# Two attention and feed-forward layers: tokens in tiles of 128 between the first attention and the experts

## The chip, the cores and the metric

The kernel runs on one core of a Trainium2 chip. Time is device time in microseconds (us). The core has a matrix engine (PE, with its weight loads shown as PEld), a vector engine (DVE), a scalar engine (ACT), a general engine (POOL), and SP, which does no arithmetic and issues transfers. ACT and POOL issue transfers too. Each engine works through its own instructions in the order in which the program emits them, and waits on semaphores for the others.

## The reference, cut to what matters

There are 16 batches of 112 tokens with 256 values, and a context of 375 rows per batch. Four stages are added to `x` in turn, each on a layernorm of it:

```python
x = x + xattn0(_layernorm(x), ctx)          # 16 heads of 64, softmax, then @ Wo + bo
x = x + ffn0(_layernorm(x))
x = x + xattn1(_layernorm(x), ctx, ctx, mask)   # one head of 256, softmax over 375
x = x + ffn1(_layernorm(x))                 # int8 product, one scale for all tokens

# ffn0
top1 = argmax(softmax(xf @ gate_w.T))       # 2 experts
masked = xf[None] * one_hot(top1).T[:, :, None]
h = relu(einsum('end,edh->enh', masked, w1) + b1[:, None, :])
routing = (einsum('enh,ehd->end', h, w2) + b2[:, None, :]).sum(0)
shared = relu(xf @ sw1 + sb1) @ sw2 + sb2   # hidden width 1024
return routing + shared
```

The expert that a token doesn't take sees zeros, so it adds a constant row, `relu(b1) @ w2 + b2`. The kernel makes those rows once (`crow`). Everything is in float32 but the last product. The scale of that product needs the maximum over all tokens, so nothing of it can begin before the last token's layernorm.

## The kernel before

**Units.** The first attention is cut into 64 units, `u = 4 * batch + k`, of four heads each (`unit`, L1007). A unit makes scores for itself (`scores`, L374), subtracts the maximum and exponentiates on ACT (`exps`, L394), divides on POOL (`divide`, L405), and in the next unit transposes the probabilities in 32x32 blocks on DVE (`unit_T`, L428) and moves the blocks between partitions by twelve transfers, on SP in most units (`unit_move`, L437). Three units later PE multiplies them with `v` (`weighted`, L462) and DVE copies the result into `oT`. Keys of the next unit and values of the unit two back are made in between (`make_kT`, `make_v`). `ctxT`, the transposed context of a batch, has three buffers.

**Work between units.** Lists `extra` and `middle` are filled by `at(u, ...)` and `mid(u, ...)` (L911 to L998) and are emitted at the end and in the middle of unit u. That written schedule sets the order on every engine. Small chains of vector work, such as a layernorm (`norm`, L241), are handed out one step at a time by `pump` while other work is emitted, and `finish` emits what is left of one.

**From attention to experts.** All activations lie in `xall`, 112 tokens of a batch on the partitions and one column block per batch. When a batch's heads are done, `attention_out` (L489) multiplies by Wo (`po`), adds to x and starts the layernorm `l1`; `ffn_turn` transposes it. `shared` (L702) runs the shared feed-forward for two batches at a time, 224 columns, eight groups in all. It runs eight hidden blocks f, each with two `ph` products and, two blocks behind, `acc` products (`Rows`, L655).

For the routed part, tokens are sorted by expert through DRAM. `sort_gate` finds the expert, `sort_place` works out the row by counting (a matmul with a triangle of ones), and `sort_put` scatters the rows with an indirect transfer. Tokens of expert 0 fill a set from the front and those of expert 1 from the back, leaving one spare slot between them, so that each slot of rows has one expert. There are three sets (`SORTED`, L48): batches 0 to 7 in 8 slots of 128 rows, 8 to 13 in 7 slots of 112, and 14 and 15 in 3 slots of 112. `sort_counts` gives each slot's expert, `slot_weights` reads it on SP (`value_load`) and loads that expert's two weight matrices of 1 MB each, double buffered; `slot_rows`, `slot_turn`, `slot_run` and `slot_store` take a slot through the expert. `sort_get` gathers a batch's rows back on POOL with the same places and `sort_add` adds them to x.

**Where the stages lie.** Slots of the first set run in units 39 to 46, with shared groups 0 to 5 in units 12 to 52, and the second attention of batches 0 to 7 is spread over units 49 to 59 (`second_1` to `second_4`, then `third`). The second set runs from step 64 to 70, the third from 71 to 73, with shared group 6 at 67 and 70. From step 75 the second attention of batches 8 to 15 is pipelined over steps (`stages`, L1084), with a quarter of shared group 7 in each of the first four; each batch is gathered four steps ahead. `keep_warm` puts idle matmuls into the last steps. Then the scale is formed and the int8 product and the output follow (L1132 on).

Of the kernel before, what the change touches and what calls it, by code (L numbers as in the profile page):

```python
# [19 lines left out]
P = 128  # L20
B, S, D = 16, 112, 256
SK = 375
# [23 lines left out]
POOL_PLACES = 7  # L46

SORTED = ((0, 8, 128), (8, 14, 112), (14, 16, 112))  # L48
# [5 lines left out]
def tile_kernel(  # L54
    ctx: ExitStack,
    tc: tile.TileContext,
    x,
    ctx_in,
# [26 lines left out]
    ctxp = ctx.enter_context(tc.tile_pool(name="ctx", bufs=3))  # L85
# [14 lines left out]
    xall = const.tile([S, B, D], F32, tag="x", name="x")  # L100
    xs = [xall[:, b, :] for b in range(B)]
# [3 lines left out]
    def load_ctx(b):  # L105
        t = late(ctxp, 3, 4, [KC, NKC, D], "ctx_nat", f"ctx{b}")
        nc.sync.dma_start(out=t, in_=ctx_in[b].rearrange("(c p) d -> p c d", p=KC))
        ctx_nat[b] = t
# [5 lines left out]
    def load_ctxT2(b):  # L114
        ctxT2[b] = ctxp.tile([P, DC, SK], F32, tag="ctxT_2", name=f"ctxT2_{b}")
        nc.sync.dma_start(out=ctxT2[b], in_=ctx_t[b])
# [6 lines left out]
    nc.sync.dma_start(out=xall[:, 0:2, :], in_=x[:, 0:2, :])  # L123
# [15 lines left out]
    def more_loads():  # L139
        load_ctxT(1)  # L140
        nc.sync.dma_start(out=xall[:, 2:4, :], in_=x[:, 2:4, :])

    def rest_of_x():
        nc.scalar.dma_start(out=xall[:, 4:, :], in_=x[:, 4:, :])
# [26 lines left out]
    half = const.tile([S, GB], F32, tag="half", name="half")  # L171
# [9 lines left out]
    def row_to_all(src, name):  # L181
        t = const.tile([S, D], F32, tag=name, name=name)
        late_loads[name] = lambda: nc.gpsimd.dma_start(out=t, in_=src.partition_broadcast(S))
        return t
# [56 lines left out]
    def norm(bs, name, on_act=False):  # L241

        n = len(bs)
        mv = small.tile([S, n, 2], F32, tag=f"mv{n}", name=f"mv_{name}_{bs[0]}")
        v = small.tile([S, n], F32, tag=f"var{n}", name=f"var_{name}_{bs[0]}")
        y = small.tile([S, n], F32, tag=f"rs_y{n}", name=f"y_{name}_{bs[0]}")
        steps = []
        for i, b in enumerate(bs):
            st = small.tile([S, 6], F32, tag="bn", name=f"bn_{name}_{b}")
            steps.append(lambda st=st, b=b: nc.vector.bn_stats(st, xs[b]))  # L250
            steps.append(lambda st=st, i=i: nc.vector.bn_aggr(mv[:, i, :], st))  # L251

        def root():
            nc.gpsimd.tensor_scalar(v, mv[:, :, 1], EPS_LN, None, ALU.add)  # L254
            nc.gpsimd.tensor_tensor(y, v, half[:, :n], ALU.pow)
# [4 lines left out]
        def rows(b, i):  # L260
            if name == "l1":
                xn = tmp.tile([S, D], F32, tag="xn1", name=f"xn_{name}_{b}")
# [7 lines left out]
            else:  # L270
                nc.vector.tensor_scalar(
                    xn, xs[b], mv[:, i, 0:1], y[:, i : i + 1], ALU.subtract, ALU.mult
# [5 lines left out]
    def transposed(dst, src, name):  # L278

        pt = gen(f"pt_{name}")  # L280
        for c in range(DC):
            nc.tensor.transpose(
                pt[:, c * S : (c + 1) * S], src[:, c * P : (c + 1) * P], ident[:S, :S]
            )
        nc.scalar.copy(dst, pt[:, : DC * S].rearrange("p (c s) -> p c s", c=DC))
# [43 lines left out]
    def q_norm(g, at_once=False):  # L329
        bs = list(range(g * GB, (g + 1) * GB))  # L330
        steps = norm(bs, "l0")
        if not at_once:
            steps.append(lambda: add_bo(bs))
        chain(("l0", g), steps)
# [3 lines left out]
    def add_bo(bs):  # L338
        for b in bs:
            nc.gpsimd.tensor_tensor(xs[b], xs[b], bo_bc, ALU.add)  # L340
# [29 lines left out]
    probs, pTs, oT = {}, {}, {}  # L370
# [91 lines left out]
    def weighted(u):  # L462
        b, k = divmod(u, UN)
        if k == 0:
            oT[b] = act.tile([P, MC, S], F32, tag="oT", name=f"oT_{b}", bufs=1)
        pa = gen(f"pa_{b}_{k}")
        pT = pTs.pop(u)
        for j2 in range(2):
# [12 lines left out]
        nc.vector.tensor_copy(  # L481
            oT[b][:, 2 * k : 2 * k + 2, :],
            pa[:, : 2 * S].rearrange("p (c s) -> p c s", c=2),
        )


    ffn_in = {}

    def attention_out(b):  # L489
        po = gen(f"po_{b}")  # L490
        for m in range(MC):
            nc.tensor.matmul(  # L492
                po[:S, :D], oT[b][:, m, :], big["wo"][:, m, :], start=(m == 0), stop=(m == MC - 1)
            )
        nc.vector.tensor_tensor(xs[b], po[:S, :D], xs[b], ALU.add)
        chain(("l1", b), norm([b], "l1"))

    def ffn_turn(b):
        g, i = divmod(b, GB)
        if i == 0:  # L500
            ffn_in[g] = tmp.tile([P, DC, GT], F32, tag="ffn_x", name=f"ffn_x_{g}")
        finish(("l1", b))
        transposed(ffn_in[g][:, :, i * S : (i + 1) * S], normed["l1", b], f"x1_{b}")

    def gate_scores(b):
        g, i = divmod(b, GB)
        sl = slice(i * S, (i + 1) * S)
        pg = gen(f"pg_{b}")
        for dc in range(DC):
            nc.tensor.matmul(  # L510
                pg[:S, :2],
                ffn_in[g][:, dc, sl],
                gw_sb[:, dc, :],
                start=(dc == 0),
                stop=(dc == DC - 1),
            )
        gs = small.tile([S, 2], F32, tag="gs", name=f"gs_{b}")
        nc.vector.tensor_copy(gs, pg[:S, :2])
# [3 lines left out]
    def sort_gate(b):  # L522
        s = sort_of[b]
        gs = gate_scores(b)
        nc.vector.tensor_tensor(second[:, b : b + 1], gs[:, 1:2], gs[:, 0:1], ALU.is_gt)

        if b == s.first:
            nc.vector.tensor_copy(seconds[:, b : b + 1], second[:, b : b + 1])
        else:
            nc.vector.tensor_tensor(  # L530
                seconds[:, b : b + 1], seconds[:, b - 1 : b], second[:, b : b + 1], ALU.add
            )

    def sort_place(b):
        s = sort_of[b]
        i = b - s.first
        pr = gen(f"pr_{b}")
        nc.tensor.matmul(
# [716 lines left out]
```

## Time and profile before

| what | us |
|---|---|
| median of 3 runs (1007.63 to 1008.91) | 1008.49 |
| the profiled execution's own time | 1008.94 |
| its span, first to last instruction | 1007.2 |
| PE, PEld busy | 960.2, 737.5 |
| DVE, ACT, POOL busy | 498.8, 470.4, 451.4 |
| start of the last unit's scores | 809.3 |
| end of the last expert slot | 927.1 |
| start of the last stage's wait for all tokens | 978.1 |

The page's time rows of 40 slices show granted PE clock 9 (0.9 or more) in all but one slice, and from 28 to 231 GB/s moved in a slice. Busy times of different engines overlap, so they don't add up to the span. A row of the stage view gives a stretch of the span and how long each engine worked in it. A row of a timeline gives start, length, engine, line, operation and tile; a bracket behind it is the idle time just before and what ended it.

### The profile page before, as it was taken

To read this page: it belongs to the slowest core of one execution; us is meant where nothing else is said; L and a number is where in the kernel's file an instruction comes from. 1 tells how busy PE (TensorE), PEld (TensorE's weight loads), DVE (VectorE), ACT (ScalarE), POOL (GpSimd) and SP (SyncE) were. 2 spreads that over 40 slices of the span, in tenths; PEclk is the share of its full clock that TensorE was granted. 3 is DMA by queue.
4 is the path that set the end of the run, shared out by engine and by line. 5 is a ranking of instruction groups with operands and counts; after the bars stand their busy time and mean duration, and the time that the engine had idled before them with its cause. 6 is when DMAs were issued, how large, how long until landed. Compare 5 with 4: busy or idle time off the path is not lost. (4 is left out here: it accounts for less than half of the span.)

```text
span 1007.2 us, 17359 instructions
## 1 busy us (share of the span) xinstructions
PE 960.2 (95%) x5829; PEld 737.5 (73%) x5829; DVE 498.8 (50%) x1263; ACT 470.4 (47%) x1257; POOL 451.4 (45%) x492
## 2 busy tenths in 40 slices
PE   8999999999999999999999999899999989998874
PEld 5777687778777777877778886667777768887653
DVE  5556735553545455454353335674765632222355
ACT  4756435653565456445344334463455641222353
POOL 4764634662465445453242224663556631013434
PEclk9999999999999999999999999999999989999998
DMA  6657312431333133244554252442433375556622
GB/s 185 165 154 201 86 39 68 99 79 28 77 86 71 39 70 79 45 129 149 163 207 149 93 156 73 125 130 59 130 73 72 77 229 205 187 205 231 199 68 74
DMA packets 117832, 119.68 MB, mean 119 GB/s; under 512 B 15422, under 2 KB 106400, under 8 KB 112384
## 3 DMA queue, kind: packets, MB, share of 16 engines
q1 hardware_dynamic: 107968, 101.53, 35.6%
q10 hardware_dynamic: 7264, 10.74, 3.6%
q0 software_dynamic: 2512, 6.30, 2.1%
q8 instruction: 47, 0.77, 0.3%
q14 instruction: 41, 0.34, 0.1%
HBM read 71.78 MB, written 8.98 MB: 80 GB/s over the span
## 5 line engine op out<-in xcount | busy, mean ns | idle before, releaser
L411 POOL TENSOR_SCALAR p<-p,rden 128x375 f32<-128x375 f32 x256 | 314.4, 1241 | 235.8 <-DVE rden L408 232.4
L399 ACT ACTIVATE p<-sc,nmax 128x375 f32<-128x375 f32 x256 | 143.1, 570 | 183.8 <-DVE nmax L390 179.9
L293 PE MATMUL pk<-ctxT,wk 128*128 128x375 f32 x512 | 191.9, 497 | 5.5 <-ACT kT L302 2.4
L314 PE MATMUL pv<-wv,ctxT 128*128 128x256 f32 (+1 forms) x768 | 186.8, 379 | 0.1
L314 PEld LDWEIGHTS pv<-wv,ctxT 128*128 128x128 f32 (+1 forms) x768 | 142.8, 187 | 47.0 <-ACT kT L302 1.2
L460 ACT COPY pT<-blk 32x384 f32<-32x384 f32 x256 | 130.0, 508 | 25.2 <-DMA pT<-blk 16.8
L432 DVE STREAM_TRANSPOSE blk<-p 128x384 f32<-128x384 f32 x256 | 132.5, 553 | 8.9 <-POOL p L411 4.9
L293 PEld LDWEIGHTS pk<-ctxT,wk 128*128 128x128 f32 x512 | 90.1, 191 | 57.4 <-issue 10.5
L390 DVE TENSOR_REDUCE nmax<-sc 128x2 f32<-128x750 f32 x128 | 111.9, 912 | 0.6 <-PE sc L382 0.4
L472 PEld LDWEIGHTS pa<-pT,v 128*64 128x64 f32 (+1 forms) x1536 | 75.0, 137 | 34.2 <-issue 14.2
L382 PE MATMUL sc<-kT,qT 64*128 64x375 f32 x512 | 98.1, 501 | 0.0
L472 PE MATMUL pa<-pT,v 128*64 128x112 f32 (+1 forms) x1536 | 89.3, 265 | 3.1 <-DVE v L327 2.5
L327 DVE COPY v<-pv 119x256 f32<-119x256 f32 x64 | 27.0, 421 | 116.3 <-PE pv L314 116.3
L302 ACT COPY kT<-pk 128x375 f32<-128x375 f32 x128 | 61.0, 477 | 46.9 <-PE pk L293 46.9
L254 POOL TENSOR_SCALAR var_l<-mv_l 112x1 f32<-112x1 f32 (+1 forms) x56 | 13.5, 240 | 125.2 <-DVE mv_l L251 97.4
L689 DVE TENSOR_SCALAR hT_sl<-ph_sl,slot_b 128x112 f32<-128x112 f32 (+1 forms) x72 | 24.6, 341 | 89.5 <-PE ph_sl L679 87.5
L382 PEld LDWEIGHTS sc<-kT,qT 64*128 64x128 f32 x512 | 43.9, 186 | 32.9 <-issue 11.7
L691 ACT ACTIVATE hT_sl<-ph_sl,slot_b 128x112 f32<-128x112 f32 (+1 forms) x72 | 25.5, 359 | 87.7 <-PE ph_sl L679 74.8
L666 PE MATMUL acc_sh<-sw,hT_sh 128*112 128x256 f32 x256 | 62.8, 380 | 3.5 <-ACT hT_sh L691 3.5
L492 PE MATMUL po<-wo,oT 128*112 128x256 f32 x256 | 57.9, 379 | 0.0
L713 POOL TENSOR_TENSOR x<-x,crow 112x256 f32<-112x256 f32 x16 | 11.3, 725 | 99.4 <-DVE x L710 72.1
L679 PE MATMUL ph_sh<-ffn_x,sw 128*128 128x224 f32 x256 | 55.7, 353 | 0.0
(204 smaller groups left out, 1279.4 us busy)
## 6 DMA issues: line engine op xcount, KB each, us to landing
pT<-blk SPq DMA_DIRECT2D x732, 48.0 KB
ctxT<-in_ctx_t SPq DMA_DIRECT2D x31, 375.0 KB
ctx<-in_ctx SPq DMA_DIRECT2D x16, 375.0 KB
ew<-in_w ACTq DMA_DIRECT2D x2, 1024.0 KB
sw<-in_sw ACTq DMA_DIRECT2D x2, 1024.0 KB
out<-y SPq DMA_DIRECT2D x8, 224.0 KB
pT<-blk ACTq DMA_DIRECT2D x36, 48.0 KB
x<-in_x ACTq DMA_DIRECT2D x1, 1344.0 KB
```

Source lines behind the costliest of these rows:

```text
L293: nc.tensor.matmul(pk[:, :SK], wk_sb[:, dc, m * P : (m + 1) * P], ctxT[b][:, dc, :], start=(dc == 0), stop=(dc == DC - 1),)
L302: nc.scalar.copy(t, pk[:, :SK])
L314: nc.tensor.matmul(pv[: KP[c], n * UD : (n + 1) * UD], ctxT[b][:, dc, c * P : c * P + KP[c]], wv_sb[:, dc, k * UD : (k + 1) * UD], start=( ...
L382: nc.tensor.matmul(sc[:, j, :SK], qT[g, m][r, i * P : (i + 1) * P], kT[b, m][r, :], start=True, stop=True,)
L390: nc.vector.tensor_reduce(nmax, sc[:, :, :SK], AX.X, ALU.max, negate=True)
L399: nc.scalar.activation(p[:, :SK], sc[:, j, :SK], AF.Exp, bias=nmax[:, j : j + 1], accum_out=den[:, j : j + 1])
L411: nc.gpsimd.tensor_scalar(p, p, rden[:, j : j + 1], None, ALU.mult)
L432: nc.vector.transpose(blocked[u][:, :, h * 32 : (h + 1) * 32], probs[u][h].rearrange("p (n k) -> p n k", k=32),)
L460: nc.scalar.copy(pT[r, :, i, :], of[r, :, i, :])
L472: nc.tensor.matmul(pa[j * DH : (j + 1) * DH, j2 * S : (j2 + 1) * S].rearrange("p (i q) -> p i q", q=QB), vv[b, k][: KP[c], c, h * DH : (h ...
L492: nc.tensor.matmul(po[:S, :D], oT[b][:, m, :], big["wo"][:, m, :], start=(m == 0), stop=(m == MC - 1))
L666: nc.tensor.matmul(self.acc[:n, i, :D], hT[:, i * n : (i + 1) * n], self.wb[:, f, :], start=(f == 0), stop=(f == FC - 1),)
```

## The change

Between the first attention's output and the experts, tokens go in 14 tiles of 128 that ignore batch borders. `xall` holds tiles in that part, and batches from the gather on.

- `oT` is a ring of 256 columns. A batch that runs over its end is copied in two pieces. `attention_out`, `ffn_turn`, `sort_gate`, `sort_place` and `sort_put` work on tiles, 14 of each, as soon as the batch that ends a tile is done.
- x is loaded twice: by pairs of batches for the first layernorm (`load_xb`, one buffer, POOL after the first) and by tiles for the residual (`load_xt`, ACT).
- The shared feed-forward runs in seven chunks of 256 columns, taken from a ring of three chunks. Chunks 0 to 3 stand in units 16, 24, 32 and 47, chunks 4 and 5 in quarters in steps 64 to 69, chunk 6 in quarters in the four steps before the second attention. `Rows` carries its two blocks behind from one quarter to the next.
- There are two sets of seven tiles, each with eight slots of 128. First and last slot of a set have a fixed expert. The second set runs in steps 70 to 77 in the order 0, 7, 1, 6, 2, 5, 3, 4; weights of slots 0 and 7 are loaded from unit 58 on, those of the others behind the run two before, and the transpose of a slot is emitted ahead of the run before it.
- Residuals return to batches through DRAM: `shared_store` writes a chunk to `x2_d` (POOL), `load_xs` reads a batch of it (POOL). `places_by_batch` writes the places of a set to DRAM by tile and reads them back by batch, both on SP. `sort_get` uses those.
- `ctxT`, and before the tail `ctxT_2` and `ctx_nat`, have two buffers instead of three; `ctxT` of batch b+2 is loaded at the end of unit 4b+5, not 4b+2.
- The second attention's pipeline begins at step 82 instead of 75.

```diff
-SORTED = ((0, 8, 128), (8, 14, 112), (14, 16, 112))
+NT = B * S // P
+SORTED = ((0, NT // 2), (NT // 2, NT))
+RING = 2 * P
+CHUNK = 2 * P
+KEPT = 3
...
-    ctxp = ctx.enter_context(tc.tile_pool(name="ctx", bufs=3))
+    ctxp = ctx.enter_context(tc.tile_pool(name="ctx", bufs=2))
...
+    xall = const.tile([P, B, D], F32, tag="x", name="x")
+    xt = [xall[:, t, :] for t in range(NT)]
+    xs_place = [b if b < B - 4 else b ^ 2 for b in range(B)]
+    xs = [xall[:S, xs_place[b], :] for b in range(B)]
+    def load_xb(g):
+        xb[g] = tmp.tile([S, GB, D], F32, tag="xb", name=f"xb_{g}", bufs=1)
+        (nc.gpsimd if g else nc.sync).dma_start(out=xb[g], in_=x[:, g * GB : (g + 1) * GB, :])
...
+    def load_xt():
+        nc.scalar.dma_start(out=xall[:, :NT, :], in_=x_tiles)
...
+    def add_bo(c):
+        sl = xall[:, 2 * c : 2 * c + 2, :]
+        nc.gpsimd.tensor_tensor(sl, sl, bo_bc.unsqueeze(1).to_broadcast([P, 2, D]), ALU.add)
...
+        nc.vector.tensor_copy(oT[:, pairs, to : to + whole], of[:, :, :whole])
+        if whole < S:
+            nc.vector.tensor_copy(oT[:, pairs, : S - whole], of[:, :, whole:])
...
+    def places_by_batch(s):
+        rows = slice(s.first * P, s.last * P)
+        bs = slice(s.first * P // S, s.last * P // S)
+        nc.sync.dma_start(
+            out=place_d[rows].rearrange("(t p) o -> p (t o)", p=P), in_=place[:, s.first : s.last]
+        )
+        nc.sync.dma_start(
+            out=batch_place[:, bs], in_=place_d[rows].rearrange("(b p) o -> p (b o)", p=S)
+        )
...
     def slot_weights(s, i, part):
-        if part == 0:
+        if i in (0, s.slots - 1):
+            slot_e[s, i] = int(i > 0)
+        elif part == 0:
             slot_e[s, i] = nc.sync.value_load(s.index[0:1, i : i + 1], min_val=0, max_val=1)
...
-            while behind:
+            while behind and fs[-1] == FC - 1:
                 self.second_layer(*behind.popleft())
...
+        sl = xall[:, 2 * c : 2 * c + 2, :]
+        nc.vector.tensor_tensor(sl, acc[:, :, :D], sl, ALU.add)
+        first_crow = crow[:, 0, :].unsqueeze(1).to_broadcast([P, 2, D])
+        nc.gpsimd.tensor_tensor(sl, sl, first_crow, ALU.add)
+    def shared_store(c):
+        rows = x2_d[c * CHUNK : (c + 1) * CHUNK]
+        nc.gpsimd.dma_start(
+            out=rows.rearrange("(j p) d -> p j d", p=P), in_=xall[:, 2 * c : 2 * c + 2, :]
+        )
+    def load_xs(b):
+        nc.gpsimd.dma_start(out=xs[b], in_=x2_d[b * S : (b + 1) * S])
...
     NU = B * UN
-    LAST = NU + 11 + B - TAIL + 5
+    FIRST_RUN = NU + 6
+    STEP_0 = FIRST_RUN + NT // 2 + 5
+    LAST = STEP_0 + B - TAIL + 5
...
+    for b in range(B - 2):
+        at(b * UN + 5, load_ctxT, b + 2)
+    for t in range(NT - 1):
+        u = done(t) * UN + UN
+        at(u + 2, attention_out, t)
+        at(u + 3, ffn_turn, t)
...
+    for c, u in enumerate((16, 24, 32, 47)):
+        at(u, shared, c)
+        at(u + 2, shared_store, c)
+        blocks.add(u)
+    s = sorts[0]
+    u = NU // 2 + UN
+    at(u, sort_counts, s)
+    at(u + 1, places_by_batch, s)
...
+    s = sorts[1]
+    order = [i // 2 if i % 2 == 0 else s.slots - 1 - i // 2 for i in range(s.slots)]
+    for j in range(2):
+        for part in range(2):
+            at(NU - 6 + 2 * j + part, slot_weights, s, order[j], part)
+    at(NU, *quarter(4, 0))
+    at(NU + 1, *quarter(4, 1))
+    at(NU + 2, attention_out, NT - 1)
+    at(NU + 2, *quarter(4, 2, 2))
+    at(NU + 3, ffn_turn, NT - 1)
+    at(NU + 3, shared_store, 4)
+    at(NU + 3, *quarter(5, 0))
+    mid(NU + 4, sort_gate, NT - 1)
+    at(NU + 4, *quarter(5, 1))
+    at(NU + 4, sort_place, NT - 1)
+    at(NU + 4, sort_counts, s)
+    at(NU + 4, sort_put, NT - 1)
+    at(NU + 4, slot_rows, s, order[0])
+    at(NU + 4, slot_rows, s, order[1])
+    at(NU + 4, *quarter(5, 2))
+    at(NU + 5, *quarter(5, 3))
+    at(NU + 5, slot_turn, s, order[0])
+    for j, i in enumerate(order):
+        u = FIRST_RUN + j
+        if j + 2 < s.slots:
+            mid(u, slot_rows, s, order[j + 2])
+        if j + 1 < s.slots:
+            mid(u, slot_turn, s, order[j + 1])
+        at(u, slot_run, s, i)
+        if j + 2 < s.slots:
+            for part in range(2):
+                at(u, slot_weights, s, order[j + 2], part)
+        at(u, slot_store, s, i)
+    at(FIRST_RUN, places_by_batch, s)
+    at(FIRST_RUN + 1, shared_store, 5)
+    for i in range(4):
+        at(STEP_0 - 4 + i, *quarter(6, i))
+    at(STEP_0, shared_store, 6)
+    for b in range(TAIL, B):
+        at(FIRST_RUN + 3 if b < 13 else STEP_0, load_xs, b)
```

## The prediction

> **What bounds the kernel now.** I read the page's shares first, then busy time by stage, then TensorE's instructions in order of time. The page says that PE is busy 95% of the span and every other engine at most half:
>
> ```profile
> PE 960.2 (95%) x5829; PEld 737.5 (73%) x5829; DVE 498.8 (50%) x1263; ACT 470.4 (47%) x1257; POOL 451.4 (45%) x492
> ```
>
> A busy PE need not be a full one, so the question is whether a unit without filler is still a solid run of matmuls. Stages next (columns: stretch, length, then busy us and count of PE, PEld, DVE, ACT, POOL, then PE clock, DMA share, GB/s):
>
> ```profile
> 0.00:809.30 809.30, 794.53 (x4788) 599.64 (x4788) 425.73 (x1050) 408.50 (x1104) 399.99 (x415) 1.00 0.39 105
> 809.30:823.30 14.00, 10.61 (x86) 7.63 (x85) 8.86 (x21) 6.67 (x18) 5.76 (x6) 1.00 0.64 206
> 823.30:834.40 11.10, 10.15 (x48) 8.64 (x48) 1.34 (x4) 3.34 (x8) 0.00 (x0) 0.69 0.79 246
> 834.40:903.00 68.60, 67.35 (x461) 60.45 (x460) 19.19 (x64) 13.48 (x37) 4.94 (x7) 1.00 0.58 210
> 903.00:927.10 24.10, 22.42 (x148) 19.66 (x148) 5.85 (x19) 4.94 (x15) 6.94 (x9) 1.00 0.68 234
> 927.10:956.80 29.70, 23.68 (x110) 17.91 (x109) 11.02 (x35) 11.46 (x28) 13.20 (x22) 1.00 0.67 188
> 956.80:978.10 21.30, 16.24 (x84) 11.34 (x84) 10.91 (x38) 11.69 (x29) 8.11 (x17) 1.00 0.24 81
> 978.10:1007.20 29.10, 15.23 (x108) 12.21 (x108) 15.96 (x35) 10.28 (x20) 12.51 (x16) 0.90 0.22 64
> ```
>
> Up to 809.3, where the last unit's scores begin, PE is idle 14.8 us in all. After it come the tail's slots (to 927.1), the second attention of batches 8 to 15 (to 978.1) and the last product. The bare units settle what work is worth before 809.3 (timeline of PE: start, length, instruction):
>
> ```profile
> 789.71 1.53 PE L382 MATMUL sc<-kT,qT 64*128 64x375 f32 x8
> ...
> 797.79 1.53 PE L382 MATMUL sc<-kT,qT 64*128 64x375 f32 x8
> ...
> 805.78 3.62 PE L492 MATMUL po<-wo,oT 128*112 128x256 f32 x16
> 809.32 1.53 PE L382 MATMUL sc<-kT,qT 64*128 64x375 f32 x8
> ```
>
> Scores follow scores after 8.1 us with no gap noted on PE, and the other engines are busy below 6 us in that time. So softmax keeps up without filler, and PE work taken out before 809.3 comes off the time. `po` costs 809.32 - 805.78 = 3.54 us.
>
> **Work removed or moved ahead of 809.3.** One shared group of 224 columns and one 128-row slot:
>
> ```profile
> 548.27 2.43 PE L679 MATMUL ph_sh<-ffn_x,sw 128*128 128x224 f32 x12
> ...
> 561.23 0.94 PE L679 MATMUL ph_sl<-slot_x,ew_(0, 5)_5061 128*128 128x128 f32 x7
> ```
> ```profile
> 460.88 1.68 PE L679 MATMUL ph_sl<-slot_x,ew_(0, 0)_4151 128*128 128x128 f32 x12
> ...
> 468.18 1.38 PE L472 MATMUL pa<-pT,v 128*64 128x112 f32 x24
> ```
>
> A group is 13.0 us. Four `acc` matmuls of it step 0.87 us and four `ph` 0.75; a chunk of 256 columns keeps the 32 `acc` (6.9) and stretches the 32 `ph` by 256/224 (6.0 to 6.9), so 13.8 us. Before 809.3 six groups (78.0) become four chunks (55.2): -22.8. The other three chunks are not gone, they come back in the tail. `po`: 15 become 13, -7.1. Two fewer transposes, gates and places there (0.20 + 0.32 + 0.20 each): -1.4. Slots of the first set stay eight of 7.3 us. Sum: **-31.3 us**.
>
> Edits costed at nothing there, with their cover. The wrapped `oT` copy is a second DVE copy in 24 units (at most 0.38 us each, the row of the whole copy); DVE works 5.3 of 8.1 us. `add_bo` and the first constant row become 7 + 7 POOL operations of 512 columns instead of 16 + 16 of 256: by the row of 112x512 (1.29 us) 18 us against 23. Seven loads of `xb`, and four stores and eight loads of `x2_d` there, are POOL issues of about 1 us (the indirect ones take 1.04) beside 5 us of divides in an 8 to 12 us unit. The added traffic, three passes of 1.8 MB, is about what two slots of 2.3 MB no longer load. With two `ctxT` buffers the load of batch b+2 is issued at the end of unit 4b+5 and read 2.8 us into unit 4b+7, so it has 8.1 + 2.8 = 10.9 us; POOL's 336 KB fill lands in 3.4 us and its 784 KB in 5.2, so 375 KB fits.
>
> `places_by_batch` is the new wait. SP stores the places, then waits for that store before it reads them back, and what follows on SP waits too. Each way it moves 896 elements of 4 bytes. **The Trainium skill (DMA: Bandwidth & Descriptors, Rules for kernel authors)** says that a non-contiguous last dimension becomes one descriptor per element, which speaks against it. No row here has such a transfer. The nearest is `gate`, 2 KB on POOL in 128 short pieces, 4.6 us; seven times as many pieces give 32 us if each piece costs in full, and 4.6 if none does. I take 6, because `b`, four times the bytes in as many pieces, takes 4.3, so pieces and bytes are not the cost. At the end of unit 37 the store queues behind 1 MB of weights on SP; transposed moves and row loads of slot 0 queue behind the wait. That row already came late (its transpose waited 1.18 us at 456.8), so I add **+3**. At 32 us it would be about +25.
>
> **The tail, from 809.3.** Before: last slot ends at 117.8, first `second_1` at 119.2, end at 197.9. After, on PE:
> - units 63 to 66: rest of 63 5.4; 64 `pa`, `pv` and a quarter of chunk 4 (3.45) 7.4; 65 with gate and place 8.4 and 1 of waiting for the moved probabilities; 66 `pa`, 0.5 for the copy, `po`, two quarters 12.2; 67 to 69 transpose, 1 of waiting for the norm, four quarters, gate, place, counts, two turns 18.1. First run at **52.5**.
> - eight runs of 7.3 and seven turns of 0.36: 60.9. Weights: 2.36 MB per slot. The busiest stretch of a slot on the trace (904.1 to 912.8) moved 299 GB/s, 7.9 us a slot against 7.66 on PE; nothing for that. The second `places_by_batch` does cost: the store sits behind 2 MB just issued, landing some 11 us after the first run, and the rows of order[3] and its weights are behind it on SP. Those rows hold the turn ahead of the third run, the weights its successor: +5. Runs end at **118.4**.
> - chunk 6 (13.8) stands while the last slot is stored, gathered (issue to landing 5.5 to 7.2), added and normed. The chain is 0.7 + 2 + 1 + 5 + 0.7 + 3 = 12.4, but bn_stats waits on DVE ahead of hT of the third quarter: +3. `second_1` of batch 8 at **135.2**, 16 later than before, where batches 8 to 13 needed only the finished middle set.
> - eight steps. The last four before took 5.3 each (21.3 for 956.8 to 978.1), the first four 7.1 to 7.4 with a shared quarter inside. Eight of 5.3 are 42.4, and POOL's store of chunk 6 with three loads behind it (about 7 us of issues and waiting in step 0) leaves +2. Steps end at 179.6; the last 29.1 are unchanged: 208.7, so **+10.8**.
>
> **The clock gate, row against rule.** A 112-row slot at full clock takes 7.1 us (839.10 to 846.22); the one that began at 823.30, after 2.97 us of idle, took 11.1 at clock 0.69. The skill (TensorE: Matmul & The Clock Gate, Part 1) lets half clock come only after an idle window of about 3.4 us. By the rule my +5 hole costs itself plus perhaps 3; by the row even a 3 us hole may. I keep +5 and put 3 into the range, since idle pieces of 0.9 to 1.2 us between 957 and 978 left the clock at 1.00.
>
> **Sum.** -31.3 + 3 + 10.8 = -17.5. The profiled execution took 1008.94 (span 1007.2 and 1.7 around it), 0.45 above the median of the runs. From the median: 1008.5 - 17.5 = **991 us**.
>
> **Rivals.**
> - *The holes are covered* (the place transfers land in under 4 us and DVE does not wait): +3, +5, +3 and +2 vanish, 978. For it: SP has 5.9 us to spare at the first run. Against: the first row load is already late in unit 38.
> - *More stalls ahead of the tail*: at 100 to 106 us PE waited for moved probabilities and `v` at a low clock while start-up loads ran; x is now loaded twice around there, and POOL queues more. Doubling such losses (14.8 us idle before) costs 10: 1001.
> - *Slower*: the read-back of places as single elements. It decides from about 15 us per transfer: each microsecond over 6 is lost twice, in unit 37 and at the first run, and 17.5 / 2 = 8.8. At 20 us: 991 + 28 = 1019. For it: the rule and 896 pieces. Against: 56 pieces for each of 16 engines, and the two POOL rows that don't grow with bytes.
>
> **Chances.** Forecast 0.56 (its own range 981 to 1000), covered holes 0.13, more stalls 0.15, slower mechanism 0.10, other losses that bring it above 1010.5 0.04, and within 0.2% of before 0.02 (0.2% is about what a measurement can tell from no change). Faster: 0.56 + 0.13 + 0.15 = 0.84; same 0.02; slower 0.14. The range leaves out the lowest part of the covered case and the slower ones: 974 to 1007.
>
> **What would show it.** Right: `po` x224 and `acc_sh` x224 records, the last unit's scores near 781, the first run 52 us later, the third run waiting for `row`, and `second_1` of batch 8 about 135 us after the scores. Wrong: PE idle before the tail well above 18 us, `pk` waiting for `ctxT`, SP's longest waits at the place transfers, or slots spaced by weights at more than 8.5 us.

## The result, and the profile after

The changed kernel takes 1022.97 us (median; 1020.83 to 1026.31), the kernel before 1008.7 on the same chip: a ratio of 1.0146, 95% interval 1.0117 to 1.0175. The forecast was 991 with 974 to 1007. So the change makes the kernel slower, and the time lies outside the range.

The profiled execution took 1026.31 us, with a span of 1024.6; that is 3.3 above its median, so spans below are compared with spans. From the page of the changed kernel, the busy times of the engines:

```profile
PE 942.5 (92%) x5613; PEld 721.2 (70%) x5613; DVE 488.6 (48%) x1249; ACT 467.1 (46%) x1241; POOL 462.8 (45%) x494
```

PE has 17.7 us less to do (942.5 for 960.2), and yet the span grew by 17.4. The work did go; about 35 us of standing still came. Where it came is in the stages (stretch, length, busy us and count of PE, PEld, DVE, ACT, POOL, then PE clock, DMA share, GB/s):

```profile
0.00:800.25 800.25, 768.92 (x4606) 577.22 (x4606) 415.93 (x1043) 404.13 (x1092) 403.50 (x407) 0.98 0.41 116
800.25:853.80 53.55, 50.39 (x311) 41.78 (x310) 18.47 (x52) 14.80 (x35) 11.49 (x13) 1.00 0.17 44
853.80:927.70 73.90, 61.43 (x396) 56.41 (x397) 15.75 (x48) 14.21 (x39) 4.75 (x7) 0.91 0.60 204
927.70:946.00 18.30, 15.76 (x65) 12.91 (x64) 3.52 (x10) 2.38 (x5) 7.65 (x11) 0.92 0.47 137
946.00:993.30 47.30, 29.54 (x131) 19.24 (x129) 19.41 (x65) 21.32 (x52) 22.92 (x40) 0.89 0.43 132
993.30:1024.60 31.30, 16.51 (x108) 13.60 (x108) 15.55 (x34) 10.28 (x20) 12.52 (x16) 0.84 0.21 59
```

The last unit's scores begin at 800.25, only 9.1 earlier than before. In 0 to 800.25 PE stands idle 31.3 us (14.8 before), and the eight runs of the tail take 73.9, 12.5 of them idle. PE's instructions in order of time show two large holes (stretches in which PE stands idle) and a smaller one:

```profile
428.42 1.53 PE L399 MATMUL sc<-kT,qT 64*128 64x375 f32 x8
...
438.01 1.53 PE L399 MATMUL sc<-kT,qT 64*128 64x375 f32 x8
...
459.41 0.66 PE L300 MATMUL pt_s<-ident,row 128*128 128x128 f32 x2 [15.37 <-DMA row<-x_s]
...
474.58 1.53 PE L399 MATMUL sc<-kT,qT 64*128 64x375 f32 x8
...
878.94 0.69 PE L300 MATMUL pt_s<-ident,row 128*128 128x128 f32 x2 [10.59 <-DMA row<-x_s]
...
964.33 0.63 PE L300 MATMUL pt_x<-ident,xn_l 112*128 112x112 f32 x2 [6.34 <-ACT xn_l L286]
```

The same stretch of the kernel before:

```profile
449.58 1.53 PE L382 MATMUL sc<-kT,qT 64*128 64x375 f32 x8
...
456.78 0.41 PE L644 MATMUL pt_s<-ident,row 128*128 128x128 f32 x2 [1.18 <-DMA row<-x_s]
...
469.49 1.53 PE L382 MATMUL sc<-kT,qT 64*128 64x375 f32 x8
```

The scores of unit 39 come at 438.01, before at 449.58, so until then 11.6 us were won. Unit 39 then takes 36.6 us against 19.9 before, and 16.7 are lost at once: PE waits 15.37 for the rows of slot 0. Between units 40 and 63 another 14.2 are won. In the tail PE waits 10.59 ahead of the third run; the rows that it waits for are those of the fourth slot in order, whose transpose is emitted there.

Both row loads stand on SP behind `places_by_batch`. SP's issues around the first (start, length, what; the length of a row of several issues holds the waits between them):

```profile
431.76 0.59 SPq L647 DMA_DIRECT2D ew_(0, 0)_4040<-in_w  x1
432.45 0.37 SPq L125 DMA_DIRECT2D ctxT<-in_ctx_t  x1
432.86 0.43 SPq L575 DMA_DIRECT2D place_d<-place  x1
444.68 0.34 SPq L578 DMA_DIRECT2D batch_place<-place_d  x1
445.07 0.55 SPq L647 DMA_DIRECT2D ew_(0, 0)_4072<-in_w  x1
445.78 11.10 SPq L462 DMA_DIRECT2D pT<-blk  x12
457.00 0.52 SPq L661 DMA_DIRECT2D row<-x_s  x1
```

From the issue of the store to that of the read-back 11.8 us pass; weights, twelve moves and the row stand behind it. The view of SP's waits counts 24.2 us for the two sets together (sum, times, longest):

```profile
SPq L578 <- DMA place_d<-place: 24.2, 2, 12.9
```

That much is a reading of the trace. Which part of it costs the time is open: SP's wait, or the transfer.

### The profile page after: what moved, and what is told of

The parts are those of the page before. It is cut to its first block, busy times and chain, and to the rows that moved or that the text cites. A ratio compares the mean times of both kernels' runs of the same rounds, so it can differ in the third digit from the quotient of the medians.

```text
span 1024.6 us, 16896 instructions
## 1 busy us (share of the span) xinstructions
PE 942.5 (92%) x5613; PEld 721.2 (70%) x5613; DVE 488.6 (48%) x1249; ACT 467.1 (46%) x1241; POOL 462.8 (45%) x494
## 5 line engine op out<-in xcount | busy, mean ns | idle before, releaser
L311 PE MATMUL pk<-ctxT,wk 128*128 128x375 f32 x512 | 194.0, 501 | 4.4 <-ACT kT L320 2.3
L449 DVE STREAM_TRANSPOSE blk<-p 128x384 f32<-128x384 f32 x256 | 132.2, 552 | 10.1 <-DMA pT<-blk 4.6
L399 PEld LDWEIGHTS sc<-kT,qT 64*128 64x128 f32 x512 | 43.9, 186 | 34.2 <-issue 13.6
L708 DVE TENSOR_SCALAR hT_sl<-ph_sl,slot_b 128x128 f32<-128x128 f32 x64 | 22.4, 350 | 86.7 <-PE ph_sl L698 86.7
L685 PE MATMUL acc_sh<-sw,hT_sh 128*128 128x256 f32 x224 | 57.1, 388 | 2.5 <-ACT hT_sh L710 1.8
L698 PE MATMUL ph_sh<-ffn_x,sw 128*128 128x256 f32 x224 | 56.3, 382 | 0.5 <-ACT ffn_x L303 0.5
L271 POOL TENSOR_SCALAR var_l<-mv_l 112x1 f32<-112x1 f32 (+2 forms) x54 | 13.1, 243 | 93.2 <-DVE mv_l L268 75.1
L368 PE MATMUL pq<-xT,wq 128*128 128x224 f32 x256 | 54.7, 357 | 0.0
L710 ACT ACTIVATE hT_sl<-ph_sl,slot_b 128x128 f32<-128x128 f32 x64 | 23.2, 367 | 63.4 <-PE ph_sl L698 52.0
L416 ACT ACTIVATION_READ_ACCUMULATOR p<-sc,nmax 128x1 f32 x256 | 51.8, 202 | 0.0
```

The lines of the kernel that those rows point to most:

```text
L311: nc.tensor.matmul(pk[:, :SK], wk_sb[:, dc, m * P : (m + 1) * P], ctxT[b][:, dc, :], start=(dc == 0), stop=(dc == DC - 1),)
L399: nc.tensor.matmul(sc[:, j, :SK], qT[g, m][r, i * P : (i + 1) * P], kT[b, m][r, :], start=True, stop=True,)
L416: nc.scalar.activation(p[:, :SK], sc[:, j, :SK], AF.Exp, bias=nmax[:, j : j + 1], accum_out=den[:, j : j + 1])
L449: nc.vector.transpose(blocked[u][:, :, h * 32 : (h + 1) * 32], probs[u][h].rearrange("p (n k) -> p n k", k=32),)
L685: nc.tensor.matmul(self.acc[:n, i, :D], hT[:, i * n : (i + 1) * n], self.wb[:, f, :], start=(f == 0), stop=(f == FC - 1),)
L698: nc.tensor.matmul(ph[:, : self.n], self.wa[:, dc, f * P : (f + 1) * P], self.src[:, dc, :], start=(dc == 0), stop=(dc == DC - 1),)
```

## The experiments

All times are medians. The kernel before was measured beside each group of runs: 1008.96 for the first four, 1008.67 for the next three, 1009.45 for the last three.

### Taking SP's wait away

`e1_split_sp` leaves the store where it is and moves the read-back, now `places_back`, seven units (in the tail five steps) later.

```diff
+    def places_back(s):
...
     at(u + 1, places_by_batch, s)
+    at(44, places_back, s)
...
     at(FIRST_RUN, places_by_batch, s)
+    at(FIRST_RUN + 5, places_back, s)
```

> The read-back of the places moves from right behind its store to unit 44 (first set) and to step 75 (second set), still on SP, so SP no longer stops for the store; nothing else changes. Theory A, the wait on SP is the loss: the hole ahead of slot 0 (15.4 us and a cold start, 16.7 against before's unit 39) and the one ahead of the third tail run (10.6 and 2.5) close, and the time falls by 25 to 30, to 993 to 998. Rival B, the rows of slot 0 are late because SP's probability moves of unit 38 and the scatter are late whatever the places do: it falls by less than 13, to 1010 or more. Rival C, the 4-byte transfers hold up the queue itself: the holes stay, since the transfers are still there, and the time stays within 5 us of 1023.

Measured: 1019.2 (ratio 1.0101, 1.0064 to 1.0137), 3.8 below the changed kernel, which is hardly more than the intervals can tell. SP no longer waits between store and weights in unit 37:

```profile
432.50 0.43 SPq L575 DMA_DIRECT2D place_d<-place  x1
432.97 0.95 SPq L651 DMA_DIRECT2D ew_(0, 0)_4071<-in_w  x1
434.08 16.13 SPq L462 DMA_DIRECT2D pT<-blk  x12
450.33 0.51 SPq L665 DMA_DIRECT2D row<-x_s  x1
```

and PE still stands, ahead of slot 0 and of the third run of the tail (timeline of PE, same kernel):

```profile
452.63 0.66 PE L300 MATMUL pt_s<-ident,row 128*128 128x128 f32 x2 [8.95 <-DMA row<-x_s]
...
874.23 0.69 PE L300 MATMUL pt_s<-ident,row 128*128 128x128 f32 x2 [9.31 <-DMA row<-x_s]
```

The wait ahead of the read-back has gone, and most of each hole stays; rival C of the expectation named both the holes and the time. But SP isn't free of the store yet. The twelve moves take 16.13 us to issue where they took 11.10, and SP's waits show why:

```profile
SPq L462 <- DMA place_d<-place: 6.4, 1, 6.4
```

In this program SP's transfers signal eight semaphores in turn, and an issue waits until the transfer before it on the same semaphore has landed. The seventh of the moves has the store's semaphore in the trace (105), and is issued as the store lands. So this run shortens SP's wait for the store and moves it; it doesn't take it away, and alone it doesn't settle the first theory, that SP's wait in its order of work is the cost. The tail does speak against it: there SP issues the rows right behind the store (859.12 behind 858.59), and PE gets them 15 us later.

`e2_split_pool` issues store and read-back on POOL, at the same places as `e1_split_sp`, so that nothing of SP's stands behind them and no issue of SP waits for the store.

```diff
-        nc.sync.dma_start(
+        nc.gpsimd.dma_start(
             out=place_d[rows].rearrange("(t p) o -> p (t o)", p=P), in_=place[:, s.first : s.last]
         )
```

> As the run before, but store and read-back are issued by POOL, whose own ring holds no expert weights, and whose landing times the profile shows. If single elements are dear, store and read-back land more than 9 us after issue here too. If the 12 to 13 us on SP were the 1 to 2 MB of weights ahead in the same queue, they land in 3 to 5 us. Time: 993 to 1000 under theory A.

Measured: 1020.44 (1.0114, 1.0074 to 1.0153; two runs). The first store lands 11.9 us after its issue; the two read-backs land in 3.2 and 6.9, so of what was expected here only the store's half came true. SP and its weights are on another queue, and yet the traffic of the whole core nearly stops for nine microseconds (stages of 3 us, columns as above, last one GB/s):

```profile
430.00:433.00 3.00, 3.00 (x14) 2.25 (x13) 0.17 (x1) 1.37 (x5) 3.00 (x3) 1.00 1.31 30
433.00:436.00 3.00, 3.00 (x18) 2.20 (x16) 0.82 (x2) 2.36 (x6) 1.72 (x2) 1.00 0.84 38
436.00:439.00 3.00, 0.35 (x4) 0.00 (x0) 0.00 (x0) 0.00 (x0) 0.00 (x0) 1.00 0.56 27
439.00:442.00 3.00, 1.40 (x24) 1.16 (x24) 2.62 (x4) 0.66 (x3) 0.00 (x0) 0.76 0.75 272
```

2 MB of weights had been issued on SP just before (428.57 and 429.78). The DMA engines have packets open (share 0.56 to 1.31) and move 27 to 38 GB/s. SP now waits for landings of its own weights and moves (5.4 us at the longest), and PE's hole is spread over the moves (3.00), `ctxT` (3.55) and the rows (4.11). The time is the same without any wait of SP for the store. That led to the second theory: the 896 single elements hold up what shares the DMA engines with them, whichever queue they come from.

### The hole in the steps

The 6.34 us at 964.33 have another cause. POOL stores the last chunk to `x2_d` and stands until that store has landed before it issues the loads of batches 13 to 15, with roots of norms behind them. `e3_later_loads` spreads these loads over the next three steps; `e4_split_and_later` does that and the split of `e1_split_sp`.

```diff
-        at(FIRST_RUN + 3 if b < 13 else STEP_0, load_xs, b)
+        at(FIRST_RUN + 3 if b < 13 else STEP_0 + b - 12, load_xs, b)
```

> The places stay as they are on SP. Only the loads of batches 13, 14 and 15 from DRAM move, from right behind the store of chunk 6 in step 82 to steps 83, 84 and 85. If POOL's wait of 6.75 us for that store causes the 6.3 us hole on PE at 958 to 964, with the cold clock after it, the time falls by 6 to 9, to 1014 to 1017. If the steps are held by something else, it falls by less than 2.

> Both edits: read-back of the places split off on SP, and loads of batches 13 to 15 one to three steps later. If the two losses are separate their gains add: 985 to 991. If the wait in step 82 was only what was left of a delay that the places caused, the sum is less than the parts, 993 to 998.

Measured: 1024.74 (1.0151, 1.0112 to 1.019) and 1018.28 (1.0092, 1.0056 to 1.0129): the same as the kernels they were made from. The hole stays (timeline of `e3_later_loads`), because POOL now waits in the next step for a load that it has just issued:

```profile
968.10 1.01 PE L300 MATMUL pt_x<-ident,xn_l 112*128 112x112 f32 x4 [7.14 <-ACT xn_l L286]
```

### The places as rows

`e5_rows_split` is `e1_split_sp` without single elements. VectorE copies the seven columns of places to FP32, TensorE turns (transposes) them into seven rows of 128, and these go to DRAM as rows of 512 bytes; eight rows of 448 bytes come back and are turned again.

```diff
+        pf = spare[:, :n]
+        nc.vector.tensor_copy(pf, place[:, s.first : s.last])
+        nc.tensor.transpose(pq[:n, :P], pf, ident)
+        pr = spare[:n, 16 : 16 + P]
+        nc.vector.tensor_copy(pr, pq[:n, :P])
-            out=place_d[rows].rearrange("(t p) o -> p (t o)", p=P), in_=place[:, s.first : s.last]
+            out=place_d[rows].rearrange("(t p) o -> t (p o)", p=P), in_=pr
...
+        nc.sync.dma_start(out=t, in_=place_d[rows].rearrange("(b p) o -> b (p o)", p=S))
...
+        nc.tensor.transpose(pq[:S, :n], t, ident[:n, :n])
+        nc.vector.tensor_copy(batch_place[:, bs], pq[:S, :n])
```

> The changed kernel with the places carried as rows: VectorE copies the 7 columns of places to FP32, TensorE turns them, the store to DRAM is 7 rows of 512 bytes in place of 896 single elements; the read-back is rows of 448 bytes and comes at unit 44 and at the sixth step of the tail (as in the split kernel), turned again by TensorE. Theory C (the 896 single elements hold the DMA engines for some 10 us wherever they are issued, and weights, moves and rows behind them come late): the holes in front of slot 0 (9 to 15 us) and of the third run of the tail (9 to 11 us) fall under 3 us, and the time is 1002 to 1008, about 15 to 20 below the changed kernel and 11 to 17 below the split one. Theory A2 (the holes come from the order of weights, moves and rows on the queues, whatever the places cost): the holes stay at 7 us and more and the time is 1015 to 1020.

Measured: 1001.4 (0.9934, 0.9919 to 0.9949). That is 21.6 below the changed kernel, 17.8 below `e1_split_sp`, which has the same schedule of store and read-back, and faster than the kernel before. In unit 38 (two stages, SP's moves, then PE's wait for slot 0 and its transpose ahead of the third run of the tail):

```profile
429.00:432.00 3.00, 3.00 (x14) 2.26 (x13) 0.00 (x0) 1.36 (x4) 3.00 (x3) 1.00 1.08 427
432.00:435.00 3.00, 3.00 (x19) 1.95 (x19) 1.83 (x5) 2.02 (x5) 1.36 (x2) 1.00 0.92 323
```
```profile
429.17 10.61 SPq L463 DMA_DIRECT2D pT<-blk  x12
```
```profile
442.15 0.41 PE L301 MATMUL pt_s<-ident,row 128*128 128x128 f32 x2 [2.65 <-DMA row<-x_s]
...
852.77 0.44 PE L301 MATMUL pt_s<-ident,row 128*128 128x128 f32 x2
```

The same weights now come at 323 to 427 GB/s, the moves take 10.61 us to issue for 16.13, the hole at slot 0 is 2.65 for 8.95, and the one ahead of the third run, 9.31 in `e1_split_sp`, is gone; the longest wait for rows in a later run is 1.50. The expectation of the second theory holds for the holes, and the time lies 0.6 below its range.

`e6_rows_behind` puts the read-back of the rows back right behind the store, so that SP waits as in the changed kernel; the edit against `e5_rows_split`:

```diff
-    at(44, places_back, s)
-    at(45, places_turn, s)
+    at(37, places_back, s)
+    at(39, places_turn, s)
...
-    at(FIRST_RUN + 5, places_back, s)
-    at(FIRST_RUN + 6, places_turn, s)
+    at(FIRST_RUN + 0, places_back, s)
+    at(FIRST_RUN + 2, places_turn, s)
```

> As e5_rows_split, but the read-back is issued right behind the store in unit 37 and at the first step of the tail, so that SyncE waits for the store's landing with weights, moves and rows behind it, as in the changed kernel. Theory C: the row store lands in about 2 us, SyncE waits 2 to 3 us, and the time is within 3 us of e5_rows_split. Theory A (the wait in SyncE's order is the cost): 8 us or more slower than e5_rows_split.

Measured: 1007.14 (0.9991, 0.9971 to 1.0011), 5.7 above `e5_rows_split`: between what the two theories expected. SP's two waits are 10.1 us together (2 to 3 each were expected), and PE's hole at slot 0 is 5.53 in place of 2.65; the tail is as long as without the wait (212.2 against 212.6). In the profiled pair 4.2 us more are lost before unit 12, among the loads at the start, which this edit doesn't touch. So by this pair about 3 of the 5.7 belong to the wait; the rest is within what such traces differ by at the start (see the last experiment). It is a cost, and a small one.

### The single elements alone

`e7_rows_plus_elements` is `e5_rows_split` with the store of single elements added, to a DRAM tile that nobody reads.

```diff
+        nc.sync.dma_start(
+            out=spare_d[rows].rearrange("(t p) o -> p (t o)", p=P), in_=place[:, s.first : s.last]
+        )
```

> As e5_rows_split, with one store of the 896 single places to a DRAM tile that nobody reads, behind each row store (unit 37 and the first step of the tail); nothing waits for it. Theory C: the holes come back (7 to 10 us at slot 0 and at the third run of the tail) and the time is 10 to 15 us above e5_rows_split. Theory A2: within 3 us of e5_rows_split.

Measured: 1014.28 (1.006, 1.0038 to 1.0081), 12.9 above `e5_rows_split`. Stages, PE's waits, and SP's issues in the tail with one of `e5_rows_split` below them:

```profile
429.00:432.00 3.00, 3.00 (x14) 2.26 (x13) 0.17 (x1) 1.36 (x5) 2.99 (x3) 1.00 0.96 383
432.00:435.00 3.00, 3.00 (x17) 2.35 (x17) 1.31 (x3) 2.54 (x6) 1.89 (x2) 1.00 1.68 209
435.00:438.00 3.00, 3.00 (x32) 2.02 (x29) 3.00 (x8) 1.54 (x5) 0.00 (x0) 1.00 0.45 74
```
```profile
447.52 0.66 PE L301 MATMUL pt_s<-ident,row 128*128 128x128 f32 x2 [7.49 <-DMA row<-x_s]
...
865.72 0.69 PE L301 MATMUL pt_s<-ident,row 128*128 128x128 f32 x2 [6.34 <-DMA row<-x_s]
```
```profile
852.86 0.40 SPq L584 DMA_DIRECT2D spare_d<-place  x1
853.30 1.56 SPq L682 DMA_DIRECT2D row<-x_s  x1
...
846.15 0.35 SPq L679 DMA_DIRECT2D row<-x_s  x1
```

Two transfers of 3.5 KB that nobody needs cost 6.5 us each, and both holes are back. That nothing waits for them, as I had expected, isn't so: in unit 38 the seventh move has the semaphore of the spare store and waits 4.8 us for its landing. But the weights behind the store land late too, by the eighth move's wait 12.0 us after their issue for 7.2 in `e5_rows_split`, and that alone would hold the rows as long. In the tail no issue waits for the spare store; the rows are issued right behind it, and PE gets them 12.4 us after the start of the issue, for at most 6.6 in `e5_rows_split`.

`e10_before_plus_elements` does the same once to the kernel before, in unit 37.

```diff
+    def spare_places():
+        nc.sync.dma_start(
+            out=spare_d.rearrange("(t p) o -> p (t o)", p=S), in_=place[:, :TAIL]
+        )
...
+        if s.first == 0:
+            at(u + 1, spare_places)
```

> The kernel before with one store of 896 single elements (its places of batches 0 to 7) to a DRAM tile that nobody reads, on SyncE's queue in unit 37, in front of set 0's slots. Theory C: PE's wait for the first slot's row goes from 1.2 to 6 to 9 us, and the time is 4 to 8 us above the kernel before. Rival (the single elements cost only where the new order of stores and weights has no slack): within 2 us.

Measured: 1015.4 (1.0058, 1.004 to 1.0076), 6.0 above the kernel before, with this line in PE's timeline, where before it waited 1.18:

```profile
462.05 0.66 PE L644 MATMUL pt_s<-ident,row 128*128 128x128 f32 x2 [5.97 <-DMA row<-x_s]
```

So the price doesn't hang on the new order of tiles, stores and weights. Together: of the 21.6 us between the changed kernel and `e5_rows_split`, 3.8 went with moving the read-back (hardly clear of the scatter) and 17.8 with the single elements; of those, the stores make 12.9 by themselves. The remaining 4.9 show in the same two holes (8.95 to 7.49, 9.31 to 6.34), not at the read-back. That was not run alone, but the trace of `e1_split_sp` shows it at 550.52 in unit 44, among weights, and the traffic goes on:

```profile
551.00:554.00 3.00, 3.00 (x34) 2.32 (x34) 1.29 (x4) 0.00 (x0) 0.00 (x0) 1.00 1.02 334
554.00:557.00 3.00, 3.00 (x14) 1.77 (x11) 3.00 (x6) 1.17 (x5) 0.00 (x0) 1.00 0.85 328
```

So it is writing single elements to DRAM that stops the traffic; reading as many doesn't. Whether their number or their size does it stays open: no run has pieces between 4 and 448 bytes, or fewer of them.

### What else could be had

`e8_rows_steps` takes the loads of batches 13 to 15 off POOL and puts POOL's addition behind the roots. `e9_rows_steps_x` also cuts the early load of x by tiles into seven.

```diff
-        nc.gpsimd.dma_start(out=xs[b], in_=x2_d[b * S : (b + 1) * S])
+        dma = nc.sync if b >= 13 else nc.gpsimd
+        dma.dma_start(out=xs[b], in_=x2_d[b * S : (b + 1) * S])
...
-        do(-3, sort_add)
...
         do(3, lambda b: third_max([b]))
+        do(-3, sort_add)
```
```diff
-        nc.scalar.dma_start(out=xall[:, :NT, :], in_=x_tiles)
+        sl = slice(2 * c, 2 * c + 2)
+        nc.scalar.dma_start(out=xall[:, sl, :], in_=x_tiles[:, sl, :])
...
-    at(6, load_xt)
+    for c in range(NT // 2):
+        at(6 + 4 * c, load_xt, c)
```

> As e5_rows_split, and the hole of the steps is aimed at: x of batches 13 to 15 is loaded from DRAM on SyncE's queue in place of GpSimd's, and GpSimd's addition of the slots' rows comes last in its step, behind the roots of the norms. Theory D (GpSimd, in order, waits 7.3 us for the last chunk's store before it may issue these loads, and the roots behind it come late: 5.4 us of hole at the transposes of x3 and a cold clock behind it): the hole falls under 2 us and the time is 4 to 7 us below e5_rows_split (994 to 998). Rival: the last chunk's rows are late whatever GpSimd does, the hole moves one step on, and the time is within 2 us of e5_rows_split.

> As e8_rows_steps, and the early load of x in token tiles is 7 loads of 2 tiles each, at units 6, 10, ... 30, in place of one of 14 tiles at unit 6. Theory: the moves of pT behind the one large load cost 2 to 4 us near 82 and 101 us, so 2 to 4 us below e8_rows_steps; rival: other loads of that stretch (the shared expert's weights) are what the moves stand behind, and it is within 1 us.

`e8_rows_steps`: 1000.88 (0.9901, 0.9871 to 0.9932), not to be told from `e5_rows_split`. The roots are in time, and the hole has moved to the transposed context, which now stands behind those loads on SP (timeline of PE):

```profile
941.11 2.81 PE L809 MATMUL pe<-ctxT,xT 128*112 128x375 f32 x4 [4.68 <-DMA ctxT<-in_ctx_t]
```

The rival had the time right but not the reason: the rows are not what is late. SP now waits 20.3 us for the store of chunk 6, and the context behind it is issued at 927.06, in `e5_rows_split` at 919.78. `e9_rows_steps_x`: 994.41 (0.9858, 0.9824 to 0.9893), the fastest of all and 14 to 15 below the kernel before. It is 6.5 below `e8_rows_steps`, where 2 to 4 were expected, but the two intervals overlap. In the traces about 3.4 of that are won before unit 12, where PE's waits of 1.33 and 1.92 for the moves, at 82 and 101, shrink to one of 1.36. That is no proof: the nine other traces of the new order have the same program up to there, and their scores of unit 12 spread over 4.8 us (counted from unit 0's); this one lies 2.3 below the lowest of them. The rest appears in the steps, where the context comes sooner than in the other profile; nothing shows that this belongs to the edit.

## Why the prediction was wrong

It missed by 32 us (1023 for 991). By its own steps:

**Work ahead of 809.3, -31.3: the mechanism right, the sum some 6 too large.** Outside unit 39 the changed kernel won 11.6 and 14.2, 25.8 in all. What is missing there lies at the start: by unit 12 one `po` less should have won 3.5, and its scores come 1.5 later than before. The rival *more stalls ahead of the tail* named that place. But it isn't a fixed cost of loading x twice: in `e5_rows_split`, the same program up to there, unit 12 comes 3.9 earlier than before. That kernel starts the last scores at 784.09, 25.2 ahead of before, and misses its 6.1 elsewhere: 2.7 in unit 39, 0.9 for the turn in unit 37, and 1.7 at the half clock in unit 50 (the last against the changed kernel). The covers for the second `oT` copy, the wider `add_bo`, the residual's way through DRAM and two `ctxT` buffers show no wait that a run pointed to.

**`places_by_batch`, +3 and +5: the step that failed.** I priced a transfer by the nearest row, the 128 short pieces of `gate` in 4.6 us, and took 6 us a transfer; the upper bound was 32. The first place transfer took 11.8 us from its issue to the read-back's, the second wait was 12.9, and the stage costs are 16.7 in unit 39 and, in the tail, runs of 74.1 (53.5 to 127.6 after the scores) where `e5_rows_split` takes 63.9. In medians the whole is 21.6, not 8 (less what rows still cost). Two things were wrong. The row was not near: seven times the pieces, written to DRAM, against a read from it. And I asked only who waits for the transfer. The cost was mostly in transfers that have nothing to do with it and merely share the DMA engines: 17.8 of it stayed when the read-back no longer stood behind the store. My own slower rival had the single elements, but in the read-back, which stops nothing, and as a wait, lost twice for each microsecond. By that rule 12 us a transfer would have given 991 + 12 = 1003.

**Row against rule.** The Trainium skill (DMA: Bandwidth & Descriptors, Rules for kernel authors) speaks of one descriptor per element, and I let the row of `gate` outweigh it. The same page says two things that I did not put beside it. Under Specifications: below 512 bytes a transfer is a read-modify-write. Under Back-pressure in remote DMA: stalled writes stall the other queues of the same DMA engine. The page tells the latter of transfers between cores, and no run here shows what happens inside an engine; but `e2_split_pool` shows just such a picture, the weights of SP's queue at 27 to 38 GB/s while POOL's elements are written. That page's rule that issuing on another engine doesn't give another set of DMA engines fits too. The rows of `e5_rows_split` are stored in pieces of just 512 bytes, so no run tests that limit.

**The tail, +10.8.** Length of each stage from the last unit's scores on, in us; the runs' +5 is part of the forecast, and the runs end with their last matmul (so 74.1 here for 73.9 above):

| stage | forecast | changed | `e5_rows_split` |
|---|---|---|---|
| to the first run | 52.5 | 53.5 | 53.1 |
| eight runs | 65.9 | 74.1 | 63.9 |
| to the first `second_1` | 16.8 | 18.2 | 16.3 |
| the steps | 44.4 | 47.2 | 48.0 |
| the last stage | 29.1 | 31.3 | 31.3 |
| sum | 208.7 | 224.3 | 212.6 |

The list of units 63 to 69 and chunk 6 as cover hold within 1.4. The steps were given +2 for POOL's store and loads; the hole is 6.34 (5.38 in `e5_rows_split`) because roots stand behind the waiting instruction, so the term was mis-sized by about 3. The last stage was called unchanged and is 2.2 longer; the same 108 matmuls take PE 16.51 at clock 0.84 for 15.23 at 0.90. Why the clock is lower there was not tried.

**The clock gate.** Cold time after a hole was put at 3. In unit 39 a hole 14.2 longer than before's cost 16.7, so 2.5 for the cold clock, and the third run took 9.8 for 7.3. Right in kind and in size.

**Chances.** Of the 32 us, 13.6 are the place term (21.6 for 8). The other 18 are the losses above, and part of the scatter: in the spans of `e5_rows_split` 6.1 ahead of the last scores (784.1 for 778 without the +3) and 8.9 after them (212.6 for 203.7 without the +5), and 3 by which that profiled execution lies under its median. I gave the slower mechanism 0.10, as something to come alone; it came with *more stalls ahead of the tail* and with longer steps, and I had no case in which two of them add up.

## What to carry to other kernels

A transfer of single elements to DRAM is to be priced by what shares the DMA engines with it, not by its bytes or by who waits for it: here 3.5 KB cost 6 us of the kernel's time even with no reader, beside 1 to 2 MB of weights. And a transfer that nobody reads may still be waited for, by an issue that takes up its semaphore. A column on the partitions becomes rows by one small transpose on TensorE; the longest wait that it brought PE was 0.99 us. Where an edit takes a wait away and the hole stays, see first whether the wait has only moved, and then look for traffic that has stopped in the same stretch, on every queue.

## What the runs showed of the hardware

The stopped traffic doesn't show on the transfer that causes it. In the trace's DMA records of `e7_rows_plus_elements`, the packets of 4 bytes (896 of them the spare store's) all start within two microseconds and take 9 ns each, while the store lands at 439.0, as SP's wait for it ends. The packets of 8192 bytes behind them on the same queue (weights) take up to eleven times as long as those ahead. Counts and mean ns of those records, by the microsecond in which they start, on the clock of the timelines:

```
us   4-byte packets      8192-byte packets
429  -                   47 at  327 ns
430  -                   50 at  326 ns
431  16 at 9 ns          12 at  312 ns
432  935 at 9 ns         23 at  343 ns
433  -                   34 at 1422 ns
434  -                    3 at 3584 ns
435  -                    5 at 1915 ns
436  2 at 9 ns            6 at  796 ns
```

In `e5_rows_split` the latter take 309 to 415 ns from 428 to 434, and in `e1_split_sp` 309 to 341 right behind the read-back's elements (554 to 556). So the share of a stage's DMA time is no measure of what it moves: 1.31 with 30 GB/s, in the stages of `e2_split_pool`.

The clock fell after a hole shorter than I had allowed for. In `e5_rows_split` PE stands from 439.5 to 442.15, 2.65 us; stages of 1 us:

```profile
441.00:442.00 1.00, 0.00 (x0) 0.00 (x0) 0.00 (x0) 0.00 (x0) 1.00 (x2) 1.00 0.52 131
442.00:443.00 1.00, 0.85 (x4) 0.60 (x5) 0.00 (x0) 0.37 (x1) 1.00 (x2) 0.74 0.51 82
443.00:444.00 1.00, 1.00 (x3) 0.61 (x2) 0.00 (x0) 0.00 (x0) 0.58 (x1) 0.50 0.77 262
```

The clock is halved at about 442.5, when PE is at work again, and stays so for 3.4 us. The rule that I weighed (TensorE: Matmul & The Clock Gate, Part 1) wants an idle window of about 3.4 us; 2.65 was enough here, as 2.97 was in the trace of before. It need not even be one gap. In each of the twelve traces all half clocks begin at whole steps of 3.413 us from one another, so the windows are fixed, and what counts is PE's busy share of the window just past. Three of them, the first from the trace of before, the others from `e5_rows_split`:

```profile
100.44:103.85 3.41, 1.25 (x14) 0.47 (x10) 3.41 (x9) 0.84 (x2) 3.41 (x3) 1.00 0.33 72
626.79:630.21 3.42, 1.09 (x7) 0.73 (x6) 2.72 (x8) 2.97 (x10) 1.94 (x3) 1.00 0.96 259
97.73:101.14 3.41, 1.48 (x12) 0.67 (x12) 3.41 (x10) 1.46 (x3) 3.41 (x3) 1.00 0.35 72
```

The first two are followed by half clock, though PE's gaps around them are 1.77 us at most; the third, with PE busy for 43% of it, is not. Over the twelve traces and up to 970 us, PE was busy for at most 43% of the window ahead of each of the 58 half clocks, and no window with less than 42% left the clock at full.
